# A chain of four modulated convolutions on one core: edge copies moved to ScalarE, the last iterations reordered on VectorE, the last product in two pieces, loads of X in three pairs

## The chip, the core and the metric

The kernel runs on one core of a Trainium2 chip. The metric is the device time of one execution in microseconds (us): the median of three runs, 475.31 us before the change (474.93 to 475.59). A core has a matrix engine (PE, with its weight loads shown apart as PEld), a vector engine (DVE, also VectorE), an activation engine (ACT, also ScalarE), a general engine (POOL, also GpSimd) and a sequencer for transfers (SP). Each has its own instruction queue, worked off in order; they wait for each other through semaphores.

## The reference, cut to what matters

Every batch element (128 of them, 64 channels by 1024 columns) goes through four modulated convolution layers (same, upsample by 2 with a blur, same, blur with downsample by 2), whose weights depend on a style vector of that element, and the result is added to the input.

```python
def _layer(x, style, w, b, mw, mb, typ):
    s = style @ mw.T + mb
    weight = SCALE * w * s[:, None, :, None]
    demod = lax.rsqrt(jnp.sum(weight * weight, axis=(2, 3)) + EPS)
    weight = weight * demod[:, :, None, None]
    ...
out = x
for i, typ in enumerate(('same', 'upsample', 'same', 'downsample')):
    out = _layer(out, style, weights[i], biases[i], mod_w[i], mod_b[i], typ)
x = x + out
```

## The kernel before

Four elements are worked on at a time: 32 quads q = 0..31 (`NQ`), two elements on the two halves of the 128 partitions, two pairs behind each other. The four layers are linear, so the kernel first makes one merged filter per element (small 64x64 matmuls: `stage1`, `stage2`, `stage3`, whose results pass through PSUM tiles psS, psR and psW into S, R and Wf) and then applies it to X. X is held in three planes (every third column, 344 columns each), and the filter is applied by five products over sums of planes, after the manner of a fast convolution. `product(q, m, ...)` is one of these: three taps, each as four matmuls on 64x64 quarters of the array and 342 columns (`NB`), written to a PSUM tile psA or, for product 4, to Y. A matmul of this type stands as two instructions in the program, so a product is 24 matmul rows on PE.

The parts of one quad that the change and the prediction speak of:

- Inputs, on DVE unless POOL is named: `in_g01` and `in_g2` make G from X (L715), `in3` makes the operand T3 (L764), `in04` the two operands T04 (L795, both pairs of elements in one instruction, or one with `PAIR[0]`/`PAIR[1]`), `in1` and `in2` the two operands T12 (L781, L786; on POOL except in the first and last quads).
- Weights on DVE: `combine_a`, `combine_b` (L715 and L712, tile H).
- Products in the order 3, 1, 2, 4, 0. `copy_m3` saves product 3 (ACT, L847), `sum1` makes y from product 1, `sum2` makes Y and y from product 2 (DVE), then product 4 accumulates in Y and product 0 in psA.
- `output(q, i, s)` scales plane i of pair s and adds the bias into the o tile (ACT, L887; one of the last two on DVE, L889), `store` sends it to HBM.
- The edge columns (three at each end of each element) are wrong in the merged form. They are computed apart, into Oe; `correct(q, planes)` copies the edge columns of o into Oc (POOL, L1169) for the first 27 quads, and `correct_all` subtracts Oe from all of these at once (DVE, L1178); for the later quads `correct` subtracts directly (L1171). `store_ends` sends Oc to HBM. `gather(q)` is `correct` for both groups of planes.

The order is written by hand (`tc.manual_schedule`): each engine gets its instructions in the order in which the Python code emits them, and waits are put in where the tiles' regions demand it. `early_turn(q)` does quads 0 to 3, `turn_of(q)` quads 4 to 28, and the code behind the loops quads 29 to 31. A turn works on several quads at once: products 2, 4 and 0 of q, products 3 and 1 of n = q+1, filter and inputs of c = q+2, the first filter stage of s = q+4. `load(c + 1, ...)` fetches X for q+3 through SP's queue, into one of two buffers; a store goes through the same queue. The transfers use eight semaphores (DMAHW0 to DMAHW7) in turn, so that a transfer waits first for the one eight before it.

At the start PE fills Y with zeros (`zeros_to_y`, L186: a zero weight times zeros), since products of the small filters accumulate there; the first matmuls on data (L223) need the parameters that the first transfers bring.

Of the kernel before, what the change touches and what calls it, by code (L numbers as in the profile page):

```python
# [55 lines left out]
K = 3  # L56
# [7 lines left out]
def kernel(  # L64
# [110 lines left out]
    NB = 342  # L175
# [618 lines left out]
            )  # L794
            nc_v.tensor_sub(t[:, pairs, :, :NJ], both(a, PL), both(b, 1))  # L795

    def product(q, m, ps, groups=range(K), alone=False):

        W, H_ = Wq[q]
        tag, i = SLOT[m]  # L800
        for g in groups:
            for s, rows in enumerate(HALF):
                for c, cols in enumerate(HALF):
                    if m in (0, 4):
                        w = W[rows, tap(m // 2, g), c, :]
                    else:
                        w = H_[rows, m - 1, g, c, :]
                    nc.tensor.matmul(  # L808
                        ps[s][cols, :NB],
                        w,  # L810
                        Ts[q, tag][rows, c, i, g : g + NB],
                        start=(g == 0 and (m == 3 or alone)),
                        stop=(g == K - 1),
                        skip_group_check=True,
                    )
# [12 lines left out]
    def banks(q):  # L828
        return A[q] if isinstance(A[q], list) else [A[q][:, s] for s in range(2)]
# [19 lines left out]
    def conv1(q, *groups):  # L849
        product(q, 1, banks(q), groups or range(K))  # L850
# [7 lines left out]
    def conv2(q, *groups):  # L858
        product(q, 2, banks(q), groups or range(K))
# [18 lines left out]
        nc_g.memset(t[:, :, :, NB:], 0.0)  # L878
    os = [t[:, :, :, :NB] for t in o_tiles] * (NQ // 2)

    def output(q, i, s, eng=nc_a):

        d3, add = td[:, q, s : s + 1], tb[:, q, s : s + 1]
        src = (banks(q)[s][:, :NB], y1w[q][:, s], Y[:, s, :NB])[i]
        dst = os[q][:, s, i]
        if eng is nc_a:
            nc_a.activation(dst, src, AF.Identity, bias=add, scale=d3)  # L887
        else:
            eng.tensor_scalar(dst, src, d3, add, op0=ALU.mult, op1=ALU.add)  # L889
# [270 lines left out]
        at, step = ((0, NB - 1), (0, NB - 2))[planes.start > 0]  # L1160
        return o[:, :, at : step + 1 : step, planes], 2 * q

    LATER_ENDS = NQ - 5

    def correct(q, planes, eng=nc_g):
        src, b = edges(q, planes)
        at = slice(b, b + 2)
        if q < LATER_ENDS:
            eng.tensor_copy(Oc[:, at, :, planes], src)  # L1169
        else:  # L1170
            eng.tensor_sub(Oc[:, at, :, planes], src, Oe[:, at, :, planes])  # L1171

    def gather(q):
        for planes in (slice(1, K), slice(0, 1)):
            correct(q, planes)

    def correct_all(n):
        nc_v.tensor_sub(Oc[:, : 2 * n], Oc[:, : 2 * n], Oe[:, : 2 * n])  # L1178
        store_ends(0, n)
# [13 lines left out]
    first = PART[0]  # L1193
    psB = [Y[:, r] for r in range(2)]
    zeros_to_y(2, 384, 6)
    zeros_to_y(2, 96, 1, False)
    nc_v.tensor_scalar_mul(mbs, mb, SCALE)
    mod_matmul(first, pm[0][0], (2,))
    nc_v.tensor_mul(wsq[T, 2], wio[2][T], wio[2][T])
    zeros_to_y(2, 256, 2, False)  # L1200
    nc_a.activation(
        ssq[:, 2, first],
        by_layer(pm[0][0], first)[:, 2],
# [137 lines left out]
    def last_factors():  # L1341
# [22 lines left out]
        14: lambda: (blur_side(0, 0), blur_side(1, 0)),  # L1364
        15: lambda: (blur_side(0, 1), blur_side(1, 1)),
        16: lambda: (blur_side(0, 2), blur_side(1, 2)),
        28: lambda: correct_all(LATER_ENDS),
    }

    def extra(*at):  # L1370
# [20 lines left out]
    def early_turn(q):  # L1391
        n, c, s = q + 1, q + 2, q + 3 + (q >= AHEAD)
        twice = q == AHEAD
        if q == 1:
            nc.sync.dma_start(Xe, x_ends)
        stage2(c)
        sum2(q)
        if q == 0:
            in_g01(n)
        if q == 1:  # L1400
            in_g2(n)
            load(n + NX)
        combine_a(n)
        combine_b(n, range(2 if q == 0 else 3))
        if q == 0:
            in_g2(n)
            load(n + NX)
        conv4(q)
        if q == 0:
            var_matmul(PART[1], var_of(PART[1]), start=False)  # L1410
            var_root(PART[1], var_of(PART[1]))
            in1(n, nc_v)
            in2(n, nc_v)
            combine_b(n, (2,))
# [36 lines left out]
        outputs(q, 1)  # L1451
        if q > 1:
            in_g2(c)
            if q < AHEAD:
                load(c + NX)
        extra(q, 1)
        sum1(n)
        if q == 0:
            in04(n)
        if q == 1:  # L1460
            in_g01(c)
        conv0(q, 1)
        if twice:
            stage1_a(s)
        else:
            stage1_b(s)
        if q == 0:
            table_3(PART[1])
            vector_Da(PART[1])
        conv0(q, 2)  # L1470
        for i in range(2):
            output(q, 0, i)
        conv2(n, 0)
        if twice:
            stage1_b(s)
        if q == 0:
            in_g01(c)
        if q == 1:
            in_g2(c)
            load(c + NX)  # L1480
        if q:
            in1(c, nc_g)
            in2(c, nc_g)
            gather(q - 1)
        extra(q, 2)
        scale3(s + 1)
        if q == AHEAD - 1:
            scale3(s + 2)
        conv2(n, 1, 2)
        for i in range(2):  # L1490
            store(q, i, slice(0, 1 if late(q) else K))

    def turn_of(q):
        n, c, s = q + 1, q + 2, q + 4
        entry = q == FIRST
        stage2(c)
        if entry:
            sum2(q)
            conv4(q)
            combine_a(n)  # L1500
            r_sums(c, nc_v)
        else:
            if q - 1 in SLOTS:
                SLOTS[q - 1][0](banks(q - 1))
            conv2(q)
            r_sums(c, nc_g)
            if q - 1 in SLOTS:
                SLOTS[q - 1][1](A[q - 1])
            sum2(q)
            in2(n, nc_g)  # L1510
        side(TABLES, q)
        for i in range(3):
            load(c + 1, slice(i, i + 1))
        stage3_b(c, open_a(n))
        if entry:
            conv0(q, 0, 1)
        else:
            combine_a(n)
            conv4(q)
        stage3_a(c)  # L1520
        combine_b(n)
        conv3(n)
        if entry:
            copy_m3(n)
            stage1_a(s)
        outputs(q, 2)
        if not entry:
            if s < NQ:
                stage1_a(s)
            copy_m3(n)  # L1530
        in04(n)
        if sharing(q):
            share_sums(c + 1)
        in_g2(c)
        side(SIDE, q)
        if q in SMALL:
            l, bs = SMALL[q]
            nc_v.memset(high(bs.stop - bs.start), 0.0)
        conv0(q, *((2,) if entry else range(K)))
        if entry:  # L1540
            conv1(n, 0, 1)
        outputs(q, 1)
        if s < NQ:
            stage1_b(s)
        in_g01(c)
        if sharing(q):
            share(c + 1, banks(q))
            share_copy(c + 1)
        outputs(q, 0)
        conv1(n, *((2,) if entry else range(K)))  # L1550
        if q in SMALL:
            small(q)
        sum1(n)
        in3(c)
        gather(q - 1)
        if s == NQ:
            in04(c)
        in1(c, nc_g)
        if s + 1 < NQ:
            scale3(s + 1)  # L1560
# [16 lines left out]
    conv3(n)  # L1577
    outputs(q, 2)
    copy_m3(n)
    in_g01(c)  # L1580
    in_g2(c)
    in3(c)
    stage3(c, 1)
    conv0(q, 0)
    conv1(n)
# [4 lines left out]
    conv0(q, 1, 2)  # L1590
    outputs(q, 0)
    for i in range(2):
        for planes in (slice(1, K), slice(0, 1)):
            correct(q - i, planes)
    conv2(n)
    sum2(n, (0,))
    combine_b(c, (1,))
    in1(c, nc_v)
    sum2(n, (1,))
    combine_b(c, (2,))  # L1600
# [47 lines left out]
        plus(i, o[:, i, 2], Y_banks, one_td, m3[:, i])  # L1648
        store(q, i, slice(2, K))
    correct(q, slice(1, K), nc_v)  # L1650
    conv0(q, *range(K))
    for i, (eng, queue) in enumerate(zip(BOTH, (nc_a, nc.sync))):
        output(q, 0, i, eng)
        store(q, i, slice(0, 1), queue)
    correct(q, slice(0, 1), nc_v)
    store_ends(LATER_ENDS, NQ)


# [74 lines left out]
```

## Time and profile before

| | |
|---|---|
| three runs | 474.93, 475.31, 475.59 us |
| the profiled execution | 475.6 us, of which the profile's span is 473.2 us |
| DVE, ACT, POOL busy | 414.8 us (88%), 311.3 us (66%), 186.0 us (39%) |
| DMA | 70.78 MB, mean 150 GB/s |
| granted TensorE clock | 0.998 |

The page gives for each engine its busy time, then the chain of work that ended last, then the costliest groups of instructions. In an answer of the timeline each row has a start in us, a duration in us, engine, line, operation, tile written and tiles read, form and count, and in brackets the idle time of the engine before it with what ended it. A row with a count merges instructions that follow each other; its start is the first one's. Ends of matmuls are modelled, so the pace of PE is read from start to start.

### The profile page before, as it was taken

How to read it: one execution, taken by the hardware profiler on the slowest of the kernel's cores; microseconds unless marked ns; L12 is line 12 of the kernel's file. 1: busy time of each engine (PE TensorE's matmuls, PEld its weight loads, DVE VectorE, ACT ScalarE, POOL GpSimd, SP SyncE). 2: the span in 40 equal slices, each digit the busy share in tenths (PEclk: the TensorE clock that was granted, in tenths of full speed). 3: DMA queues.
4: the chain of work that ended last, by engine and by line, in shares of the span. 5: the costliest groups of instructions: out<-in, count | busy, mean ns of one | idle time of the engine just before them, and what ended most of it. 6: DMA issues, size and time to landing. Idle time of an engine off the chain costs nothing. (4 is left out here: it accounts for less than half of the span.)

```text
span 473.2 us, 26920 instructions
## 1 busy us (share of the span) xinstructions
PE 466.0 (98%) x11996; PEld 343.0 (72%) x11996; DVE 414.8 (88%) x676; ACT 311.3 (66%) x711; POOL 186.0 (39%) x268
## 2 busy tenths in 40 slices
PE   9999999999999999999999999999999999999996
PEld 7987778777767779677877677766677676676653
DVE  5899989778989989998999987898898889889995
ACT  5566566577776667665777756687666777766364
POOL 4634241763448642243433333323334433243310
PEclk9999999999999999999999999999999999999999
DMA  5226444554445453344534545444555544455225
GB/s 178 93 96 212 165 158 145 153 158 139 157 152 157 153 181 126 122 153 153 158 133 153 167 124 176 145 150 151 143 175 161 180 138 149 142 154 160 98 91 183
DMA packets 52835, 70.78 MB, mean 150 GB/s; under 512 B 6128, under 2 KB 50928, under 8 KB 52720
## 3 DMA queue, kind: packets, MB, share of 16 engines
q1 hardware_dynamic: 52496, 68.84, 45.7%
q8 instruction: 94, 1.54, 1.4%
q14 instruction: 21, 0.17, 0.1%
q10 hardware_dynamic: 224, 0.23, 0.1%
HBM read 35.03 MB, written 34.01 MB: 146 GB/s over the span
## 5 line engine op out<-in xcount | busy, mean ns | idle before, releaser
L808 PE MATMUL psA<-T,H 64*64 64x342 f32 x2304 | 186.7, 448 | 0.0
L808 PEld LDWEIGHTS psA<-T,H 64*64 64x64 f32 x2304 | 88.9, 134 | 47.8 <-issue 2.1
L715 DVE SCALAR_TENSOR_TENSOR G<-X 128x1378 f32<-128x1378 f32 (+2 forms) x65 | 78.3, 1211 | 0.2
L487 POOL TENSOR_TENSOR S<-S 128x128 f32<-128x128 f32 x28 | 20.9, 745 | 140.1 <-ACT S L402 140.0
L781 POOL TENSOR_TENSOR T<-G 128x688 f32<-128x688 f32 x28 | 46.4, 1658 | 63.4 <-DVE G L715 59.4
L808 PE MATMUL Y<-T,Wf 64*64 64x342 f32 x768 | 62.6, 454 | 1.1 <-DVE Y L715 1.1
L808 PE MATMUL psA<-T,Wf 64*64 64x342 f32 x768 | 63.6, 448 | 0.0
L402 ACT ACTIVATE R<-psR,tC 128x448 f32<-128x448 f32 x63 | 36.5, 630 | 35.6 <-PE psR L509 20.8
L402 ACT ACTIVATE psW<-psA 128x128 f32<-128x128 f32 x100 | 19.3, 269 | 54.4 <-PE psA L624 50.3
L715 DVE SCALAR_TENSOR_TENSOR Y<-m,psA 128x342 f32<-128x342 f32 x62 | 32.2, 519 | 25.7 <-PE psA L808 24.6
L795 DVE TENSOR_TENSOR T<-G 128x1376 f32<-128x1376 f32 (+1 forms) x33 | 52.6, 1593 | 0.0
L402 ACT ACTIVATE Wf<-psW,t 128x256 f32<-128x256 f32 (+2 forms) x76 | 32.7, 480 | 29.1 <-PE psW L624 28.9
L764 DVE TENSOR_TENSOR T<-X 128x688 f32<-128x688 f32 x32 | 51.4, 1606 | 0.0
L786 POOL TENSOR_TENSOR T<-G 128x688 f32<-128x688 f32 x28 | 47.2, 1685 | 0.0
L509 PE MATMUL psR<-S,E 64*64 64x64 f32 (+1 forms) x1472 | 46.7, 238 | 0.0
L431 PEld LDWEIGHTS psS<-wd,w2n 64*64 64x64 f32 x1120 | 34.4, 133 | 13.4
L808 PEld LDWEIGHTS Y<-T,Wf 64*64 64x64 f32 x768 | 28.3, 132 | 20.5 <-DVE Y L715 1.3
L509 PEld LDWEIGHTS psR<-S,E 64*64 64x64 f32 x1472 | 38.9, 134 | 5.2 <-ACT psR L532 0.2
L887 ACT ACTIVATE o<-psA,tb,td 128x342 f32<-128x342 f32 x63 | 37.2, 651 | 5.0 <-PE psA L808 5.0
L808 PEld LDWEIGHTS psA<-T,Wf 64*64 64x64 f32 x768 | 29.0, 134 | 15.1 <-ACT m L1643 0.2
L887 ACT ACTIVATE o<-Y,tb,td 128x342 f32<-128x342 f32 x62 | 36.1, 641 | 4.8 <-PE Y L808 2.9
L887 ACT ACTIVATE o<-y,tb,td 128x342 f32<-128x342 f32 x62 | 38.6, 681 | 0.0
(186 smaller groups left out, 840.0 us busy)
## 6 DMA issues: line engine op xcount, KB each, us to landing
out<-o SPq DMA_DIRECT2D x191, 172.0 KB, 2.3
X<-in_x SPq DMA_DIRECT2D x150, 172.0 KB, 3.1
X<-in_x SPq DMA_DIRECT2D x14, 516.0 KB, 4.7
par<-in_params SPq DMA_DIRECT2D x3, 192.0 KB, 3.8
Xe<-in_x_ends SPq DMA_DIRECT2D x1, 192.0 KB, 3.8
out<-o ACTq DMA_DIRECT2D x1, 172.0 KB, 2.2
out<-Oc SPq DMA_DIRECT2D x1, 162.0 KB, 3.4
par<-in_params SPq DMA_DIRECT2D x1, 160.0 KB, 2.7
```

The source lines that it names most:

```text
L402: nc_a.activation(dst, src, AF.Copy, scale=f)
L431: nc.tensor.matmul(ps[r][cols, at * C : (at + n) * C], weight[rows], wd[c if r == 0 else 1 - c][rows, taps], start=first, stop=last, skip_ ...
L487: nc_g.tensor_add(t[:, :, 2], t[:, :, 2], t[:, :, 0])
L509: nc.tensor.matmul(dst[r][cols], weight[rows], st[c if r == 0 else 1 - c][rows, slots, :], start=False, stop=last, skip_group_check=True,)
L715: nc_v.scalar_tensor_tensor(out, x, f, y, op0=ALU.mult, op1=op)
L764: nc_v.tensor_sub(t[:, pairs, 0, :NJ], plane(X, 3, pairs), plane(X, 1, pairs))
L781: eng.tensor_add(t[:, :, 0, :NJ], plane(g, 2), plane(g, 1))
L786: eng.tensor_sub(t[:, :, 1, :NJ], plane(g, 2), plane(g, 1))
L795: nc_v.tensor_sub(t[:, pairs, :, :NJ], both(a, PL), both(b, 1))
L808: nc.tensor.matmul(ps[s][cols, :NB], w, Ts[q, tag][rows, c, i, g : g + NB], start=(g == 0 and (m == 3 or alone)), stop=(g == K - 1), skip_ ...
L887: nc_a.activation(dst, src, AF.Identity, bias=add, scale=d3)
```

## The change

Five edits in one:

1. `gather` for quads 0 to 25 is done by ACT (a copy), right behind the outputs of the same quad, and no longer by POOL one turn later. `LATER_ENDS` falls from 27 to 26, so quad 26 is subtracted directly, and `correct_all` comes in turn 27 instead of 28.
2. `load(c + 1, ...)`: the three pairs of transfers of a turn, which stood together near the start of the turn, stand apart: ahead of the outputs of plane 2, behind them, and behind those of plane 1.
3. DVE's order from turn 28 on: of `in04(30)` only the first pair stays in turn 28; `in3(31)` and the second pair of `in04(30)` come ahead of `in_g01(31)`, and `in_g2(31)` comes later, between two steps of `combine_b(31)`, ahead of `in1(31)`.
4. The last product (product 0 of quad 31) is done in two pieces: first the columns 0 to 87 and 254 to 341 ("sides", one access pattern with two runs of 88), with their outputs, stores, the last `correct` and `store_ends`, then the 166 columns between ("middle") with theirs.
5. The same number of zero columns is written to Y at the start in more and narrower matmuls: 96 columns in 3 pieces instead of 1, 256 in 4 instead of 2.

```diff
-    def product(q, m, ps, groups=range(K), alone=False):
+    WHOLE = slice(0, NB)
+    SIDES, MIDDLE = 88, slice(88, NB - 88)
+
+    def columns(v, at):
+        if at != SIDES:
+            return v[..., at]
+        ap = [list(d) for d in v.ap]
+        return bass.AP(v.tensor, v.offset, [*ap[:-1], [ap[-1][0] * (NB - SIDES), 2], [ap[-1][0], SIDES]])
+
+    def product(q, m, ps, groups=range(K), alone=False, at=WHOLE):
...
-                        ps[s][cols, :NB],
+                        columns(ps[s][cols], at),
                         w,
-                        Ts[q, tag][rows, c, i, g : g + NB],
+                        columns(Ts[q, tag][rows, c, i, g:], at),
...
-    def output(q, i, s, eng=nc_a):
+    def output(q, i, s, eng=nc_a, at=WHOLE):
...
-    LATER_ENDS = NQ - 5
+    LATER_ENDS = NQ - 6
...
-        if q < LATER_ENDS:
-            eng.tensor_copy(Oc[:, at, :, planes], src)
+        if eng is nc_a:
+            eng.copy(Oc[:, at, :, planes], src)
...
-            correct(q, planes)
+            correct(q, planes, nc_a if q < LATER_ENDS else nc_g)
...
-    zeros_to_y(2, 96, 1, False)
+    zeros_to_y(2, 96, 3, False)
...
-    zeros_to_y(2, 256, 2, False)
+    zeros_to_y(2, 256, 4, False)
...
-        28: lambda: correct_all(LATER_ENDS),
+        NQ - 5: lambda: correct_all(LATER_ENDS),
...
-        for i in range(3):
-            load(c + 1, slice(i, i + 1))
+        load(c + 1, slice(0, 1))
...
         outputs(q, 2)
+        load(c + 1, slice(1, 2))
...
         outputs(q, 1)
+        load(c + 1, slice(2, 3))
...
         outputs(q, 0)
+        if q < LATER_ENDS:
+            gather(q)
...
-        gather(q - 1)
+        if q > LATER_ENDS:
+            gather(q - 1)
         if s == NQ:
-            in04(c)
+            in04(c, PAIR[0])
...
     copy_m3(n)
+    in3(c)
+    in04(n, PAIR[1])
     in_g01(c)
-    in_g2(c)
-    in3(c)
...
     combine_b(c, (1,))
+    in_g2(c)
     in1(c, nc_v)
...
-    conv0(q, *range(K))
-    for i, (eng, queue) in enumerate(zip(BOTH, (nc_a, nc.sync))):
-        output(q, 0, i, eng)
-        store(q, i, slice(0, 1), queue)
-    correct(q, slice(0, 1), nc_v)
-    store_ends(LATER_ENDS, NQ)
+    for at in (SIDES, MIDDLE):
+        product(q, 0, banks(q), at=at)
+        for i, (eng, queue) in enumerate(zip(BOTH, (nc_a, nc.sync))):
+            output(q, 0, i, eng, at)
+            queue.dma_start(
+                columns(out[q, :, i, :NO], at), columns(o_tiles[q % 2][:, i, 0], at)
+            )
+        if at == SIDES:
+            correct(q, slice(0, 1), nc_v)
+            store_ends(LATER_ENDS, NQ)
```

The first place is DVE's queue at the end of turn 28 and in the code behind the loops (the rows between, which only make y, Y and H of quads 29 and 30, are left out by quoting two stretches). Before:

```order
L715 SCALAR_TENSOR_TENSOR G_8406<-X_102 128x2x344
L1178 TENSOR_TENSOR Oc<-Oc,Oe 128x324
L715 SCALAR_TENSOR_TENSOR G_8406<-X_102 128x2x689
L715 SCALAR_TENSOR_TENSOR y_29_8443<-psA_8310,m_29_8402 128x684
L764 TENSOR_TENSOR T_30_8445<-X_102 128x688
L795 TENSOR_TENSOR T_30_8449<-G_8406 128x1376
L715 SCALAR_TENSOR_TENSOR Y<-m_29_8402,psA_8310 128x342 x2
```

and now, on the same engine at the same place:

```order
L715 SCALAR_TENSOR_TENSOR G_8422<-X_102 128x2x344
L715 SCALAR_TENSOR_TENSOR G_8422<-X_102 128x2x689
L715 SCALAR_TENSOR_TENSOR y_29_8459<-psA_8324,m_29_8418 128x684
L764 TENSOR_TENSOR T_30_8461<-X_102 128x688
L795 TENSOR_TENSOR T_30_8465<-G_8422 128x688
L715 SCALAR_TENSOR_TENSOR Y<-m_29_8418,psA_8324 128x342 x2
```

Ahead of the Y of quad 29 stands one instruction fewer, and `in04` (L795) has half its columns. The second place is DVE's queue behind the Y of quad 30, where the inputs of the last quad are made; before:

```order
L715 SCALAR_TENSOR_TENSOR Y<-m_30_8576,psA_8559 128x342 x2
L715 SCALAR_TENSOR_TENSOR H_8510<-Wf_8509,H_8510 128x384
L781 TENSOR_TENSOR T_31_8657<-G_8578 128x2x344
L867 TENSOR_TENSOR y_30_8619<-y_30_8619,psA_8559 128x684
L715 SCALAR_TENSOR_TENSOR H_8510<-H_8510,Wf_8509 128x384
L786 TENSOR_TENSOR T_31_8657<-G_8578 128x2x344
L795 TENSOR_TENSOR T_31_8715<-G_8578 128x688
L1614 SCALAR_TENSOR_TENSOR y_31_8680<-psA_0_8662,times,m_31_8679 128x342
```

and now:

```order
L715 SCALAR_TENSOR_TENSOR Y<-m_30_8592,psA_8575 128x342 x2
L715 SCALAR_TENSOR_TENSOR H_8526<-Wf_8525,H_8526 128x384
L715 SCALAR_TENSOR_TENSOR G_8597<-X_103 128x2x344
L781 TENSOR_TENSOR T_31_8674<-G_8597 128x2x344
L877 TENSOR_TENSOR y_30_8635<-y_30_8635,psA_8575 128x684
L715 SCALAR_TENSOR_TENSOR H_8526<-H_8526,Wf_8525 128x384
L786 TENSOR_TENSOR T_31_8674<-G_8597 128x2x344
L795 TENSOR_TENSOR T_31_8732<-G_8597 128x688
L1628 SCALAR_TENSOR_TENSOR y_31_8697<-psA_0_8679,times,m_31_8696 128x342
```

The G of `in_g2(31)` has come in between. The third place is the end of the program, with the semaphores that each row waits for: first ACT's last rows before, then now.

```order
L887 ACTIVATE o_141<-psA_0_8662,tb,td 128x342 [waits DMAHW0_49,PE_49]
L892 DMA out<-o_141 128x344 [waits DMAHW4_49,Activation_49]
```

```order
L897 ACTIVATE o_141<-psA_0_8679,tb,td 128x2x88 [waits DMAHW0_49,PE_49]
L1669 DMA out<-o_141 128x2x88 [waits DMAHW4_49,Activation_49]
L897 ACTIVATE o_141<-psA_0_8679,tb,td 128x166 [waits DMAHW4_49,DVE_49,PE_49]
L1669 DMA out<-o_141 128x166 [waits DMAHW7_49,Activation_49]
```

Then DVE's last rows now (before, one row of 128x342 stood between the two of Oc):

```order
L1181 TENSOR_TENSOR Oc<-o_141,Oe 128x4x2 [waits DVE_49]
L899 TENSOR_SCALAR o_141<-psA_1_8680,td,tb 128x2x88 [waits DMAHW1_49,PE_49]
L1181 TENSOR_TENSOR Oc<-o_141,Oe 128x4 [waits DVE_49,Activation_49]
L899 TENSOR_SCALAR o_141<-psA_1_8680,td,tb 128x166 [waits DMAHW5_49,DVE_49,PE_49]
```

and SP's last transfers now:

```order
L1669 DMA out<-o_141 128x2x88 [waits DMAHW5_49,DVE_49]
L1193 DMA out<-Oc 128x72 [waits DMAHW6_49,DVE_49,Pool_49]
L1669 DMA out<-o_141 128x166 [waits DMAHW5_49,DMAHW0_49,DVE_49]
```

Each of the two last outputs has become two, and the second of each waits for the semaphore of a transfer that the first did not wait for. On PE the product's two pieces wait as follows:

```order
L818 MATMUL psA_0_8679<-T_31_8732,Wf_8525 64x2x88 [waits Activation_49]
L818 MATMUL psA_1_8680<-T_31_8732,Wf_8525 64x2x88 [waits DVE_49]
L818 MATMUL psA_0_8679<-T_31_8732,Wf_8525 64x166 [waits Activation_49]
L818 MATMUL psA_1_8680<-T_31_8732,Wf_8525 64x166 [waits DVE_49]
```

The middle's matmuls wait for ACT and for DVE a second time.

More of the change, by code (lines that the diff above doesn't have):

```diff
@@ L879 @@
     os = [t[:, :, :, :NB] for t in o_tiles] * (NQ // 2)
-    def output(q, i, s, eng=nc_a):
+    def output(q, i, s, eng=nc_a, at=WHOLE):
         d3, add = td[:, q, s : s + 1], tb[:, q, s : s + 1]
-        src = (banks(q)[s][:, :NB], y1w[q][:, s], Y[:, s, :NB])[i]
-        dst = os[q][:, s, i]
+        src = columns((banks(q)[s], y1w[q][:, s], Y[:, s])[i], at)
+        dst = columns(os[q][:, s, i], at)
         if eng is nc_a:
@@ L1549, in turn_of @@
         outputs(q, 0)
+        if q < LATER_ENDS:
+            gather(q)
         conv1(n, *((2,) if entry else range(K)))
@@ L1554, in turn_of @@
         in3(c)
-        gather(q - 1)
+        if q > LATER_ENDS:
+            gather(q - 1)
         if s == NQ:
-            in04(c)
+            in04(c, PAIR[0])
         in1(c, nc_g)
@@ L1592 @@
     for i in range(2):
-        for planes in (slice(1, K), slice(0, 1)):
-            correct(q - i, planes)
+        gather(q - i)
     conv2(n)
```

## The prediction

> **What bounds the kernel now.** I read the page's busy times first, then PE's waits, then a table of stretches, then the timeline of one turn, of the last three quads and of the first 5 us.
>
> ```profile
> span 473.2 us, 26920 instructions
> PE 466.0 (98%) x11996; PEld 343.0 (72%) x11996; DVE 414.8 (88%) x676; ACT 311.3 (66%) x711; POOL 186.0 (39%) x268
> ```
>
> PE is busy for all but 7.2 us of the span. Its waits, in the order of their sum:
>
> ```profile
> PE Y L808 <- DVE Y L715: 1.1, 1, 1.1
> PE Y L186 <- DVE eps L156: 1.0, 1, 1.0
> PE psW L624 <- issue: 0.8, 2, 0.6
> ```
>
> There are three, together 2.9 us; the rest is the stretch behind PE's last matmul. By stretch (length, then busy time of PE, PEld, DVE, ACT, POOL):
>
> ```profile
> 418.50:432.40 13.90, 13.90 (x392) 9.77 (x384) 12.11 (x19) 8.88 (x21) 5.07 (x7) 1.00 0.48 149
> 432.40:447.17 14.77, 13.66 (x281) 9.24 (x273) 14.54 (x18) 8.51 (x19) 5.34 (x5) 1.00 0.39 129
> 447.17:458.50 11.33, 11.32 (x168) 6.58 (x172) 10.92 (x20) 4.85 (x9) 1.42 (x4) 1.00 0.27 95
> ```
>
> In a turn of the loop (first row) PE is never idle, at full clock. In the second row, which runs into quad 29, it lacks 1.11 us: that is the wait for Y. So an edit pays only there, in the first microseconds, or behind the last matmul; elsewhere it can only do harm.
>
> **The loop: edge copies and loads, 0 us.** One turn in the timeline:
>
> ```profile
> 384.90 1.19 ACT L887 ACTIVATE o<-psA,tb,td 128x342 f32<-128x342 f32 x2
> 387.89 1.16 ACT L402 ACTIVATE R<-psR,tC 128x448 f32<-128x448 f32 x2 [0.91 <-PE psR L509]
> 389.35 0.94 PE L624 MATMUL psA<-R,w0s 64*64 64x192 f32 x24
> 2.60 0.20 ACT L158 ACTIVATE one<-one 128x1 f32<-128x1 f32 x1
> L402 ACT ACTIVATE psW<-psA 128x128 f32<-128x128 f32 x100 | 19.3, 269 | 54.4 <-PE psA L624 50.3 <-issue 4.1
> ```
>
> The two copies of 8 and 4 columns come behind the outputs of plane 0 (first row). No such copy on ACT is in the trace; it lies between the 0.20 us of one column and the 0.27 us of 128, nearer the first: 0.4 to 0.54 us a turn, and with a wait of each for its predecessor's end perhaps 0.7. Queued behind them are the two copies of wd and then R, ahead of which ACT idles 0.91 us until PE delivers psR: that idle time is the cover. Were it gone, PE would wait for R only after another 0.30 us (R ends at 389.05, its matmuls start at 389.35). POOL loses the work, but no wait of PE ends on POOL. So 0; if the copies cost 1.5 us instead, some 0.3 us in each of 22 turns.
>
> The loads move behind stores in SP's queue:
>
> ```profile
> 382.40 0.87 DVE L715 SCALAR_TENSOR_TENSOR G<-X 128x688 f32<-128x688 f32 x1
> 383.20 1.25 ACT L887 ACTIVATE o<-y,tb,td 128x342 f32<-128x342 f32 x2
> 386.53 4.53 SPq L147 DMA_DIRECT2D X<-in_x  x6
> X<-in_x SPq DMA_DIRECT2D x150, 172.0 KB, 3.1
> ```
>
> The six transfers are issued at the start of a turn, for a quad whose first reader (`in_g2`, as at 382.40) comes two periods of 13.90 us later, at 410.2. Moved behind the outputs of plane 1 (second row, one period later: 397.1 to 398.4) the last pair is issued by 399.2 and lands 3.1 us after that: still 8 us early. The stores between are late by the issue of one pair, about 0.8 us, and their tile is written again two turns later. 0 us.
>
> **DVE's order at the end, -0.6 us.**
>
> ```profile
> 445.12 0.94 PE L624 MATMUL psW<-R,w0s 64*64 64x128 f32 x24
> 443.09 3.04 DVE L795 TENSOR_TENSOR T<-G 128x1376 f32<-128x1376 f32 x1
> 446.05 1.06 DVE L715 SCALAR_TENSOR_TENSOR Y<-m,psA 128x342 f32<-128x342 f32 x2
> 447.17 1.96 PE L808 MATMUL Y<-T,Wf 64*64 64x342 f32 x24 [1.11 <-DVE Y L715]
> 438.62 0.49 DVE L1178 TENSOR_TENSOR Oc<-Oc,Oe 128x324 f32<-128x324 f32 x1
> 436.15 1.58 DVE L795 TENSOR_TENSOR T<-G 128x1376 f32<-128x1376 f32 x1
> 461.35 0.87 DVE L795 TENSOR_TENSOR T<-G 128x688 f32<-128x688 f32 x1
> ```
>
> PE's wait for Y (fourth row) has ahead of it on DVE the whole `in04(30)`, 3.04 us beside POOL's work where the same form alone takes 1.58. Half of it saves 1.58 - 0.87 = 0.71; without `correct_all` (0.49) the queue starts up to that much earlier. Y is then done 0.7 to 1.2 us earlier, and PE can start when its own work ahead ends, 445.12 + 0.94 = 446.06: gain 1.1, the whole wait (0.7 at the least). What is late next is the queue behind the Y of quad 30:
>
> ```profile
> 450.90 2.37 DVE L715 SCALAR_TENSOR_TENSOR G<-X 128x1378 f32<-128x1378 f32 x2
> 426.12 1.58 DVE L715 SCALAR_TENSOR_TENSOR G<-X 128x1378 f32<-128x1378 f32 x1
> 458.53 0.87 DVE L781 TENSOR_TENSOR T<-G 128x688 f32<-128x688 f32 x1
> 462.30 1.06 DVE L1614 SCALAR_TENSOR_TENSOR y<-psA,times,m 128x342 f32<-128x342 f32 x2
> 463.71 1.93 PE L808 MATMUL psA<-T,H 64*64 64x342 f32 x24
> ```
>
> `in_g2(31)` costs 2.37 - 1.58 = 0.8 us and now stands there, ahead of `in1` (third row), and I allow 0.1 for `in1`, which now waits for its predecessor's end. DVE has no gap from there to the y of quad 31, which ended at 463.36; product 2 of that quad overwrites its psA and started at 463.71. Of the 0.9 us, 0.35 is slack, and 0.5 becomes a new wait of PE. Net -0.6; ends 0 (0.7 gained, and the new wait no smaller) and -1.1 (no new wait).
>
> **The last product in two pieces, +1.9 us.** Before:
>
> ```profile
> 468.97 0.17 DVE L1171 TENSOR_TENSOR Oc<-o,Oe 128x8 f32<-128x8 f32 x1
> 469.12 0.64 ACT L887 ACTIVATE o<-psA,tb,td 128x342 f32<-128x342 f32 x1 [2.24 <-PE psA L808]
> 469.18 0.63 DVE L889 TENSOR_SCALAR o<-psA,td,tb 128x342 f32<-128x342 f32 x1
> 470.28 0.40 SPq L1183 DMA_DIRECT2D out<-Oc  x1
> out<-Oc SPq DMA_DIRECT2D x1, 30.0 KB, 2.0
> DMA to landing us min/median/max: 1.8/2.0/2.5
> ```
>
> The last row is for the ten transfers from 463 us on. The last one issued lands at 470.28 + 2.0 = 472.28, and the program ends 0.94 us later. The intent of two pieces is that the sides' outputs and stores run while PE does the middle. The order's rows forbid it. ACT issues the sides' store behind a wait for DMAHW4, and its very next output, the middle's, waits for DMAHW4 again: an engine has no need to wait twice for one count, so the second is the count that this store adds when it lands. DVE's middle output waits in the same way for DMAHW5, the semaphore of SP's store of the sides, and PE's middle matmuls wait a second time for ACT and DVE. The sides' access pattern spans columns 0 to 341, which holds the middle: the program takes the two for overlapping. So the middle may not be written before the sides have landed.
>
> From 469.18: sides 0.46 us (0.63 less 166 columns at the 342's rate of about 1 ns, so that 176 remain), issue 0.03, landing 2.0, then 0.05, middle 0.45, issue 0.03, landing 2.0: 469.18 + 5.02 = 474.20, against 472.28: +1.9. With 1.8 us for both landings +1.5, with 2.5 for both +2.9. PE's middle (half a product, whose row lasts 1.93 us) is over before the first landing, and ACT's half is earlier, since its sides don't queue behind the Oc row. [...] The sides' runs are 352 B. The trace shows no cost of that: Oc with runs of 240 B landed in 2.0 us, like the stores of 172 KB. [...]
>
> **More zeros, +0.1 us.**
>
> ```profile
> 0.97 1.58 PEld L186 LDWEIGHTS Y<-Z 64*64 64x64 f32 x56 [0.97 <-DVE eps L156]
> 2.77 0.29 PEld L223 LDWEIGHTS psM<-par_s 128*64 128x64 f32 x4 [0.22 <-DMA par_s<-in_params_s]
> 3.18 0.73 PEld L186 LDWEIGHTS Y<-Z 64*64 64x64 f32 x16
> 4.13 0.22 PEld L258 LDWEIGHTS psM<-ssq,q 64*64 64x64 f32 x4 [0.22 <-issue]
> ```
>
> 56 rows at 28 ns fill PE until 2.55, and the parameters arrive 0.22 us later; 16 more rows cost 0.45 less what narrower ones save, so they overrun by up to 0.23. The second lot, 16 rows at 46 ns, becomes 32 at 28 (+0.17) ahead of another gap of 0.22. Together 0.40 - 0.22: between 0 and 0.2 late at 4.13, from which the start's chain of dependent steps goes on. A gain is not in sight, since the columns are the same.
>
> **Sum.** 0 - 0.6 + 1.9 + 0.1 = +1.4 us. The profiled execution took 475.6 us (2.4 outside its span) and would take 477.0; it lies 0.3 above the median of the runs shown, so the median goes to 475.31 + 1.4 = 476.7 us.
>
> **The rivals.**
>
> *The pieces overlap after all* (not slower). If the second waits were for counts long reached, as DVE's for DMAHW1 ahead of its sides is, the sides are out at 469.64, their store and Oc's leave SP by 470.4, the middle's is issued at about 470.45 and lands at 472.45, +0.2, and with the other terms -0.3: 475.0. It decides if the middle's output waits less than about 0.5 us. For it: ACT's output before also waited for a transfer (DMAHW0), and its 2.24 us ended with PE's product, not with that. Against it: the repeated wait on ACT. 0.11.
>
> *The loads in pairs free the code's own fetches.* PE's 0.8 us of "issue" in L624 are waits for nothing that the profile shows; if they come from the traffic of six loads at once and go with it, and the pieces overlap as well, 475.0 - 0.8 = 474.2. Nothing in the rows ties them to the loads. 0.06.
>
> *ACT's copies push R* beyond PE's product: 22 turns at 0.1 to 0.3 us, +2 to +7 on top: 479 to 483. It begins when the two copies exceed 0.91 + 0.30 = 1.2 us; twice the dearest near row is 0.54. 0.09.
>
> **How the numbers follow.** The forecast has 0.74. Its own range from the bounds: -1.1 + 1.5 + 0 = +0.4 to 0 + 2.9 + 0.2 = +3.1, 475.7 to 478.4; both ends need every term at its end. For 8 in 10 over all cases I take 475.4 to 478.0. A difference of 0.2% (0.95 us) is about what can be told from none: of the forecast's 0.74, 0.64 lies above 476.26 and 0.10 below; with the third rival slower is 0.73. Same: 0.10 + 0.08 of the first rival = 0.18. Faster: 0.06 + 0.03 of the first rival = 0.09.
>
> **What would show it.** The landing: DVE's last output of 166 columns with some 2 us idle ahead, ended by a transfer of o, and the chain of waits ending in it instead of in PE. The DVE order: product 4 of quad 29 without its 1.11 us, and a wait of about 0.5 us ahead of product 2 of quad 31. The loop: periods of 13.90 us as before, R still waiting for PE. Wrong it would be if DVE's last two outputs stand within 1 us of each other, or if a turn's period is longer.

## The result, and the profile after

The changed kernel took 483.8 us (median of five runs, 483.1 to 485.5) where the kernel before took 475.6 beside it: a ratio of 1.0167, 95% interval 1.0146 to 1.0187, or +7.9 us. The prediction was 476.7 (475.4 to 478.0): slower, as forecast, but by more than five times as much (+1.4 predicted). The profiled execution took 485.45 us, of which the span is 483.6. Its page:

```profile
span 483.6 us, 26990 instructions
PE 473.0 (98%) x12052; PEld 378.1 (78%) x12052; DVE 414.5 (86%) x678; ACT 319.0 (66%) x764; POOL 174.2 (36%) x216
DMA out<-o 1%; DVE o L1628 0%; DVE o L899 0%; DVEq L899 0%; DVE Oc L1181 0%
q8 instruction: 94, 1.54, 1.4%
out<-o SPq DMA_DIRECT2D x190, 172.0 KB, 2.7
X<-in_x SPq DMA_DIRECT2D x150, 172.0 KB, 3.7
```

The third row is the chain that ended last: it now runs through a landing of o, as forecast. But that landing is 0.6% of the span. In the last two rows the transfers are slower: the median landing of an X load went from 3.1 to 3.7 us, that of a store from 2.3 to 2.7. And PEld is busy for 35 us more, with 56 weight loads more.

The waits of the changed kernel (engine, tile, line and what ended them: sum, times, longest), those of PE, PEld and the last outputs:

```profile
PE psA L818 <- DVE Ve L1136: 1.5, 1, 1.5
PE psA L624 <- issue: 1.1, 3, 0.5
PE psR L509 <- issue: 0.9, 3, 0.5
PEld Y L818 <- issue: 2.2, 4, 0.8
PEld psA L624 <- issue: 2.2, 5, 0.7
PEld psA L818 <- POOL R L641: 1.7, 1, 1.7
PE psA L818 <- ACT o L897: 0.4, 1, 0.4
DVE o L899 <- DMA out<-o: 2.6, 1, 2.6
```

The wait for Y of quad 29 is gone. New are the tail's waits (last two rows) and, in the loop, more waits for "issue", that is for nothing that the profile shows. They look small, but a table of stretches shows where the time went. Three turns of the changed kernel (length, then busy time of PE, PEld, DVE, ACT, POOL, clock, share of the transfers, GB/s):

```profile
342.09:356.62 14.53, 14.03 (x383) 11.39 (x382) 12.46 (x20) 10.02 (x25) 4.87 (x5) 1.00 0.50 149
371.07:385.13 14.06, 14.06 (x385) 13.71 (x385) 11.67 (x19) 10.12 (x25) 4.01 (x5) 1.00 0.50 147
208.94:226.06 17.12, 15.65 (x421) 11.09 (x416) 13.62 (x22) 10.08 (x25) 5.47 (x5) 1.00 0.44 135
```

Each stretch runs from one quad's product 4 to the next quad's, and I name the turn by the later one: 22, 24 and 13. A turn that took 13.90 takes 14.53 and 14.06, and turn 13 took 15.44 before. From the first product 4 (31.14 us) to that of quad 28 the changed kernel needs 410.2 us, the one before 403.3 (29.07 to 432.41): between these two profiles 6.9 us of the loss lie in the loop, which I had priced at nothing.

### The profile page after: what moved, and what is told of

Read it like the earlier page. It is cut to its first block, busy times and chain, and to the rows that moved or that the text cites. A ratio compares the mean times of both kernels' runs of the same rounds, so it can differ in the third digit from the quotient of the medians.

```text
span 483.6 us, 26990 instructions
## 1 busy us (share of the span) xinstructions
PE 473.0 (98%) x12052; PEld 378.1 (78%) x12052; DVE 414.5 (86%) x678; ACT 319.0 (66%) x764; POOL 174.2 (36%) x216
## 3 DMA queue, kind: packets, MB, share of 16 engines
q8 instruction: 94, 1.54, 1.4%
## 5 line engine op out<-in xcount | busy, mean ns | idle before, releaser
L818 PE MATMUL psA<-T,H 64*64 64x342 f32 x2304 | 191.2, 449 | 1.6 <-DVE Ve L1136 1.5
L818 PEld LDWEIGHTS psA<-T,H 64*64 64x64 f32 x2304 | 105.2, 133 | 37.3 <-issue 2.1
L818 PE MATMUL psA<-T,Wf 64*64 64x342 f32 (+2 forms) x792 | 66.2, 439 | 0.6 <-ACT o L897 0.4
L795 DVE TENSOR_TENSOR T<-G 128x1376 f32<-128x1376 f32 (+1 forms) x34 | 52.7, 1550 | 0.0
L509 PE MATMUL psR<-S,E 64*64 64x64 f32 (+1 forms) x1472 | 50.2, 238 | 0.7 <-issue 0.7
L509 PEld LDWEIGHTS psR<-S,E 64*64 64x64 f32 x1472 | 45.1, 134 | 4.2 <-issue 0.9
L818 PEld LDWEIGHTS Y<-T,Wf 64*64 64x64 f32 x768 | 34.0, 132 | 16.6 <-issue 2.2
L431 PEld LDWEIGHTS psS<-wd,w2n 64*64 64x64 f32 x1120 | 38.9, 133 | 9.8
L818 PEld LDWEIGHTS psA<-T,Wf 64*64 64x64 f32 x792 | 34.8, 133 | 12.4 <-ACT o L897 0.7
L897 ACT ACTIVATE o<-psA,tb,td 128x342 f32<-128x342 f32 (+1 forms) x64 | 37.6, 646 | 7.1 <-PE psA L818 4.2
L624 PEld LDWEIGHTS psA<-R,w0s 64*64 64x64 f32 x1000 | 35.2, 134 | 3.9 <-issue 0.6
```

Of the source, the lines that this page charges most:

```text
L431: nc.tensor.matmul(ps[r][cols, at * C : (at + n) * C], weight[rows], wd[c if r == 0 else 1 - c][rows, taps], start=first, stop=last, skip_ ...
L509: nc.tensor.matmul(dst[r][cols], weight[rows], st[c if r == 0 else 1 - c][rows, slots, :], start=False, stop=last, skip_group_check=True,)
L624: nc.tensor.matmul(dst[r][cols], weight[rows], t[rows, c, slots, :], start=first, stop=last, skip_group_check=True,)
L818: nc.tensor.matmul(columns(ps[s][cols], at), w, columns(Ts[q, tag][rows, c, i, g:], at), start=(g == 0 and (m == 3 or alone)), stop=(g == ...
```

## What the code's fetches show

The transfer queue "instruction" of the page (q8: 94 transfers, 1.54 MB, so 16 KB each) brings PE's code, as I read it: PE has 12,052 matmuls and as many weight loads, 24,104 in all and so 256 to a transfer. I set PE's stalls inside the loop (over 0.14 us, read from start to start) beside the number of the instruction that came late, counted from the first (with PE's 126 waits and 3 drains), modulo 256, and beside the end of the last such transfer. Some of the 18 stalls of the changed kernel:

```
stall us           length  instruction mod 256   last code transfer, us
145.81 -> 146.11   0.30    194                   143.05 - 144.69
221.18 -> 222.92   1.74    195                   220.34 - 221.24
279.52 -> 280.18   0.66    193                   277.87 - 278.79
355.87 -> 356.62   0.75    193                   354.42 - 355.34
412.82 -> 413.19   0.37    193                   410.68 - 411.57
```

All stalls stand at the same place in a block of 256 instructions (190 to 195), and end 1.2 to 1.7 us after a block has landed (a few fall in two parts, the first ending 0.8 to 0.9 us after it). The reverse holds too: between 100 and 445 us the changed kernel passes this place 72 times and the kernel before 73 times, never less than 1.2 us after the last landing, and where the block landed early there is no stall. I read this as PE having run out of code. The five loop stalls of the profile before (its two "issue" waits of L624 among them) stand at 193 and 194 too: 2.0 us in sum, against 8.3 us now. The stall of 1.74 us, which the list of waits lays to DVE and POOL, is one of them: the work named had simply ended last. Of the 72 code transfers between 100 and 445 us, 12 start when PE has fewer than 140 instructions left to that place; of 73 before, 5. What else moves then are X and the outputs: in the kernel before a short block of stores and, after a pause, the rest of the stores and then the six loads; in the changed kernel loads and stores in turn, in one stretch from about 5 to 13 us of a turn. So far this is a reading of traces. The runs tested it. Where I speak of the phase, I mean where in a turn the place 193 falls; a turn is three blocks long, so the phase stays from turn to turn until other code comes in. In both kernels the transfer of a block starts 51 to 292 instructions ahead of the place where it is needed.

## The experiments

Each kernel was run beside the one before on the same chip; ratios carry their 95% interval, and a difference in us is the ratio's distance from 1 times 475. The first four are the edits alone.

**Loads in pairs alone.**

```diff
-        for i in range(3):
-            load(c + 1, slice(i, i + 1))
+        load(c + 1, slice(0, 1))
...
         outputs(q, 2)
+        load(c + 1, slice(1, 2))
...
         outputs(q, 1)
+        load(c + 1, slice(2, 3))
```

> The kernel before, with the six loads of a turn issued as three pairs and nothing else. Theory 'late code': in the changed kernel PE's new stalls in the loop (0.2 to 0.75 us each, released by nothing that the profile shows) follow fetches of PE's code that start late, because the pairs and the stores between them make one unbroken block of transfers; then this edit alone carries the loop's loss: +4 to +6 us, 479.5 to 481.5, periods of 14.0 to 14.6 us in turns 14 to 28, and PE's issue waits 3 us or more in sum. Rival 'late R' (the two copies on ACT): no change here, 475.0 to 476.0 and periods of 13.90. Rival 'both together': below +2 here and below +2 for the copies alone.

Measured 479.0 us, 1.0086 (1.0069 to 1.0102): +4.1 us. The periods of turns 21 to 27 are 13.94 to 14.35, as in this row of its stretches:

```profile
350.82:365.08 14.26, 14.26 (x392) 12.52 (x385) 12.06 (x19) 9.80 (x23) 4.81 (x7) 1.00 0.50 156
```

This is turn 23. PE shows as busy throughout: its modelled ends swallow a stall of 0.22 us at 352.7. The weight loads tell it: they are spread over 12.5 us in place of 9.8, which I read as PE running close to the end of its code. Eleven stalls, 4.9 us, all at 192 to 194 of a block. The size is that of "late code", but PE's list of waits gives only 1.9 us of them as "issue" where I expected 3 or more, and the stalls are not in every turn from 14 on.

**Edge columns on ACT alone.**

```diff
-        if q < LATER_ENDS:
-            eng.tensor_copy(Oc[:, at, :, planes], src)
+        if eng is nc_a:
+            eng.copy(Oc[:, at, :, planes], src)
```

> The kernel before, with the edge columns copied by ACT (and correct_all one turn earlier) and nothing else. 'Late code': 475.0 to 476.0, periods of 13.90. 'Late R': 479 to 481, with PE waiting for R in some 20 turns. 'Both together': below 477.5 here and for the loads alone.

Measured 473.7 us, 0.9976 (0.9962 to 0.9990): -1.1 us, faster than any of the theories had it. "Late R" falls. ACT's rows of one turn:

```profile
384.55 0.37 ACT L1169 COPY Oc<-o 128x8 f32<-128x8 f32 x2
384.82 1.01 ACT L402 ACTIVATE wd<-w3x,tA 128x320 f32<-128x320 f32 x2
386.49 1.16 ACT L402 ACTIVATE R<-psR,tC 128x448 f32<-128x448 f32 x2 [0.66 <-PE psR L509]
```

A pair of copies holds the next row up by 0.27 us, and ACT still idles 0.66 us ahead of R. Of the gain, 0.4 us is PE's wait for Y of quad 29 (its period is 14.36 in place of 14.75): `correct_all` has left that turn.

**The last product in two pieces alone.**

```diff
+    for at in (SIDES, MIDDLE):
+        product(q, 0, banks(q), at=at)
```

> The kernel before, with the last product in two pieces and nothing else. Theory 'a landing in between': +1.9 as predicted, +2.6 if the landings last as long as in the changed kernel: 477.2 to 478.1, with DVE's last output idle 2.0 to 2.7 us until a transfer of o lands. Rival 'the pieces overlap': 475.3 to 475.8.

Measured 477.2 us, 1.0041 (1.0026 to 1.0056): +1.9 us.

**More zeros alone.**

```diff
-    zeros_to_y(2, 96, 1, False)
+    zeros_to_y(2, 96, 3, False)
...
-    zeros_to_y(2, 256, 2, False)
+    zeros_to_y(2, 256, 4, False)
```

> The kernel before, with the zeros of Y in more and narrower matmuls and nothing else. The changed kernel's profiled run was 2.1 us late at the first product (31.14 against 29.07), and its matmuls kept the slow pace until about 8 us where those of before were at the fast pace from about 4.7. Theory 'the zeros cause it': 477 to 478, in all runs. Rival 'it varies by itself from run to run': 475.3 to 476.0 in the median, with single runs of this kernel and of the one before up to 2 us apart and a lower granted clock in the longer ones. My prediction's term was +0.1 (0 to 0.2).

Measured 475.6 us, 1.0017 (1.0004 to 1.0030): +0.8 us. The time lies in the rival's range, but the kernel before ran at 474.8 beside it, so a small cost is left. Most of the 2.1 us by which the changed kernel's profile was late is chance. The 32 rows of the first blur matmuls show it, in the kernel before, in the changed one, and in the kernel with pieces apart (below), whose start is that of before:

```profile
4.69 1.32 PE L382 MATMUL Y<-par,idb 64*64 64x192 f32 x32
```

```profile
5.13 2.41 PE L382 MATMUL Y<-par,idb 64*64 64x192 f32 x32
```

```profile
4.86 2.41 PE L382 MATMUL Y<-par,idb 64*64 64x192 f32 x32
```

With one and the same code at the start they took 1.32 to 2.41 us in nine profiles, and quad 0's product 4 came at 29.07 to 30.41; with more zeros, in five profiles, at 29.44 to 31.14. The profile of before happened to be the earliest of all.

**Loads in pairs and more zeros**, then **loads in pairs and copies on ACT**: the diffs above, two at a time.

> The kernel before with loads in pairs and the zeros in more matmuls. The single edits measured +4.2 and +0.8 on 474.8. Theory 'late code, by phase': PE's code arrives in blocks of 256 instructions, a turn holds about three of them, and the 64 instructions that the zeros add move the turn against the blocks, so that another fetch meets the pairs' transfers: more than the sum, 481 to 483, with issue waits in nearly each turn from 14 on, as in the changed kernel. Rival 'additive': 479.5 to 480.1, and the loop's periods as with the loads alone (14.2 to 14.35 in turns 21 to 27, 13.9 in most others).

Measured 481.2 us, 1.0141 (1.0117 to 1.0165): +6.7 us, where the two alone make +4.9. The 14 loop stalls make 7.8 us, the longest 1.94.

> The kernel before with loads in pairs and the edge columns copied by ACT. The single edits measured +4.2 and -1.0. 'Late code, by phase': neither moves PE's code, so they add up: 477.5 to 478.5. Rival 'both together' (ACT's copies delay the stores that the pairs stand behind): 480 to 482, periods like the changed kernel's 14.1 to 14.7 from turn 19 on.

Measured 477.4 us, 1.0053 (1.0032 to 1.0075): +2.5 us, and the two alone make +3.0. So not the copies but the zeros make the paired loads dearer, by 1.8 us, which is just outside the intervals of the three runs (about 1.5 together).

**The changed kernel with its loads together again** (the first diff undone).

> The changed kernel with the six loads of a turn issued together again, as before; everything else as changed. 'Late code': the loop's loss goes, periods of 13.90 again, and what is left is copies -1.0, pieces +2.4, zeros +0.8 and DVE's order about -0.6: 476.0 to 477.0. Rival 'another edit makes half of the loss': 478 to 480.

Measured 476.1 us, 1.0031 (1.0016 to 1.0047): +1.5 us. Two loop stalls are left, 0.6 us. The loads' share of the changed kernel is 7.9 - 1.5 = 6.4 us.

**DVE's order alone.**

```diff
-            in04(c)
+            in04(c, PAIR[0])
...
-    in_g2(c)
-    in3(c)
+    in3(c)
+    in04(n, PAIR[1])
...
     combine_b(c, (1,))
+    in_g2(c)
```

> The kernel before with DVE's new order from turn 28 on and nothing else (correct_all stays in turn 28). Predicted term -0.6, ends -1.1 and 0; without the move of correct_all the gain of 1.1 shrinks to some 0.7 and the new wait of 0.5 ahead of product 2 of quad 31 stays: 474.3 to 474.8 against 474.8. Rival 'no new wait': 473.7 to 474.1.

Measured 474.2 us, 0.9987 (0.9972 to 1.0001): -0.6 us, a little more than expected of this edit with `correct_all` left in its place (474.3 to 474.8), and the interval reaches no change. Its one wait of PE past the first us:

```profile
PE Y L808 <- DVE Y L715: 0.4, 1, 0.4
```

**Loads in pairs with fewer zeros**, and **fewer zeros alone**: PE's code shifted by 64 instructions the other way.

```diff
-    zeros_to_y(2, 384, 6)
+    zeros_to_y(2, 384, 3)
...
-    zeros_to_y(2, 256, 2, False)
+    zeros_to_y(2, 256, 1, False)
```

> The kernel before with loads in pairs and FEWER zero matmuls at the start (384 columns in 3 pieces instead of 6, 256 in 1 instead of 2), which takes 64 instructions out of PE's code, as many as the more zeros add. Theory 'late code, by phase': in the loads-alone run the three fetches of a turn became due about 0.9, 6.7 and 10.2 us into the turn and waited 1.5 to 2.7 us; 64 instructions less move them to about 2.3, 7.1 and 10.9 us, where the first finds no traffic and the others have up to 0.7 us less of it ahead: issue stalls of 0 to 0.1 us in turns 19 to 27, loop loss 0 to 1.5 us instead of 4.2, 474.4 to 476.4. Rival 'phase is no matter': +4.2 as with the loads alone, 478.3 to 479.3.

Measured 479.9 us, 1.0102 (1.0080 to 1.0124): +4.8 us, far outside what I expected. Yet the turns for which I had worked it out came as expected. Two stretches of it, turns 15 and 23:

```profile
239.52:254.48 14.96, 14.03 (x393) 12.56 (x388) 12.88 (x21) 9.78 (x23) 4.86 (x6) 1.00 0.46 145
354.09:367.99 13.90, 13.90 (x392) 9.77 (x384) 12.11 (x19) 9.78 (x23) 5.07 (x7) 1.00 0.52 167
```

Turns 19 to 27 have no stall over 0.14 us. The loss moved to turns 8 to 17: eight stalls, 6.4 us. Between lie turns with edge matmuls, which add code and so shift the block against the turn once more; I had carried the phase of the last turns over to all. The phase has a say in where the stalls fall, and in the three phases tried the paired loads lost in one part of the loop or another. It isn't alone in this: loads in pairs with copies on ACT have the phase of the loads alone, and their stalls stand partly in other turns (none in 21 and 22, one in 19).

> The kernel before with FEWER zero matmuls at the start and nothing else. Theory 'each zero matmul costs': the more zeros measured +0.8, so as many fewer give -0.3 to -0.8: 474.1 to 474.6. Rival 'the narrow ones alone are at fault': 474.9, no change; rival 'fewer matmuls let PE fall idle and get its fast pace later': 475.5 to 477.

Measured 474.3 us, 0.9992 (0.9978 to 1.0005): -0.4 us, not told from no change. No stall in the loop.

**The last product in pieces that do not overlap.**

```diff
+    LEFT, RIGHT, MIDDLE = slice(0, 88), slice(NB - 88, NB), slice(88, NB - 88)
...
+    for part in ((LEFT, RIGHT), (MIDDLE,)):
+        for at in part:
+            product(q, 0, banks(q), at=at)
```

> The kernel before with the last product in pieces whose regions do not overlap: columns 0 to 87, 254 to 341 and 88 to 253 as three runs, each with matmuls, outputs and stores of its own. Theory 'the overlapping pattern makes the last outputs wait for a landing': the wait of 2 us on DVE is gone, and what is left is 24 more matmul rows and two more stores ahead of the last: 474.7 to 475.7, against 477.2 for the two pieces. Rival 'two steps of store cost two landings in any case': 476.8 to 477.6.

Measured 475.8 us, 1.0024 (1.0011 to 1.0037): +1.1 us. The landing is out of the way, in DVE's last rows and PE's:

```profile
469.57 1.17 PE L814 MATMUL psA<-T,Wf 64*64 64x166 f32 x24 [1.36 <-ACT o L893]
468.98 0.64 DVE L895 TENSOR_SCALAR o<-psA,td,tb 128x88 f32<-128x88 f32 x2
470.79 0.45 DVE L895 TENSOR_SCALAR o<-psA,td,tb 128x166 f32<-128x166 f32 x1 [0.90 <-PE psA L814]
```

What remains is a wait of PE for ACT, 1.36 us: its middle matmuls write the psA tile that ACT has just been reading, other columns of it.

**ACT copies and DVE's order together** (their diffs above).

> The kernel before with the edge columns copied by ACT and DVE's new order at the end: the two edits that measured faster alone (-1.0 and -0.7). Additive: 473.0 to 473.5, and the wait of PE for Y of quad 29 gone entirely. Rival 'both gain from the same wait of PE for Y' (correct_all's 0.49 us and half of in04): -1.0 to -1.2 in sum, 473.7 to 473.9.

Measured 473.7 us, 0.9974 (0.9961 to 0.9986): -1.2 us (a gain of 0.7 to 1.9), the rival's value: both draw on the one wait for Y, which is gone from PE's waits. The interval reaches the additive -1.7 as well, so the time alone does not decide it.

By then the cause lay in the loads, but their traffic and their place among the stores were still one. **Loads in pairs, more zeros, and the loop's loads left out** (the diff is against the kernel with pairs and more zeros); then **six loads together, but later in the program**:

```diff
-        load(c + 1, slice(0, 1))
...
-        load(c + 1, slice(1, 2))
...
-        load(c + 1, slice(2, 3))
```

> The kernel with loads in pairs and more zeros (481.2, stalls of 0.2 to 1.9 us in most turns from 10 on), with the loads of X in turns 4 to 28 left out, so that these quads work on old data; PE's code is the same. Theory 'the traffic of X delays the code': no stalls of over 0.3 us in the loop, periods of 13.90 in turns 19 to 27, 474.0 to 476.0. Rival 'something else in PE's code or in the stores': stalls stay, 479 or more.

Measured 476.6 us, 1.0020 (1.0001 to 1.0040): +1.0 us instead of +6.7. One loop stall over 0.14 us is left, of 0.4 us. Its turn 23, with 80 GB/s instead of some 150:

```profile
349.37:363.27 13.90, 13.90 (x393) 9.77 (x385) 12.12 (x19) 9.80 (x23) 5.08 (x7) 1.00 0.23 80
```

The median is 0.6 us above what I expected; I had not counted what more zeros cost without any loads in pairs, +0.8 alone.

```diff
         outputs(q, 1)
+        for i in range(3):
+            load(c + 1, slice(i, i + 1))
```

> The kernel before with the six loads of a turn still together, but issued behind the outputs of plane 1, where the last pair stands in the changed kernel. Theory 'one unbroken stretch of transfers, with a fetch due early in it': the fetch that is due about 10.2 us into the turn then stands behind six loads and the stores of plane 1 and waits over 3 us: stalls in turns 19 to 27, periods over 14.2, 478 to 486. Rival 'it is the alternation of loads and stores in pairs': 13.90, 474.5 to 475.5.

Measured 476.1 us, 1.0015 (0.9995 to 1.0035): +0.7 us, with an interval that reaches no change. The stalls that my theory expected did not come; the rival's 13.90 came, and its time nearly. Its turn 23, and its page's row of the loads with the median landing:

```profile
347.92:361.82 13.90, 13.90 (x392) 9.77 (x385) 11.74 (x19) 9.80 (x23) 5.07 (x7) 1.00 0.54 172
X<-in_x SPq DMA_DIRECT2D x150, 172.0 KB, 4.0
```

As much traffic, in one block and with slower landings (4.0 us, against 3.5 with the pairs alone), but only two loop stalls, of 0.5 us each. So slow landings are not enough. But the edit moved the traffic less than it seems to: each load comes nearly a whole turn later, and so lands at nearly its old place in a turn. Counted from product 4, the six are issued at 8.4 to 11.2 us, now ahead of the last two stores; in the kernel before at 9.7 to 13.8, behind them; with the pairs alone at about 5, 8 and 11, between the stores. So the stalls come with the traffic of X as the pairs place it. Whether it is the alternation with the stores or the earlier start that makes them is not shown, nor why the code waits longer there.

The loop's length in the profiles, from the first product 4 to that of quad 28, parts the kernels in the same way: 406.2 to 410.2 us in the five with pairs, 400.9 to 403.3 us in the twelve without. The kernel before is the longest of the twelve; the kernel with DVE's order alone, whose loop is the same, took 401.4. So the loop stalls of one profile are those of one execution, and such a profile tells a loop's time to about 2 us.

**The parts that gain: ACT copies, DVE's order, fewer zeros.**

> The kernel before with the edge columns on ACT, DVE's new order at the end and fewer zero matmuls: the parts that measured below 1.0 alone or together (0.9974 and 0.9992). Additive: 0.9966, 473.0 to 473.6. Rival 'they don't add, since the zeros move the code against the loop': 473.7 to 474.9.

Measured 473.1 us, 0.9940 (0.9920 to 0.9961): -2.8 us against the kernel before. The medians differ by 2.0 us only, since the runs of before scattered more than elsewhere (473.4 to 477.9). Its median is the lowest of all kernels run, and within what I expected of the sum. Its list of PE's waits has one row, the first wait of the program:

```profile
PE Y L186 <- DVE eps L156: 1.0, 1, 1.0
```

## Why the prediction was wrong

- **The loop's loads, 0 us: the step that failed.** I asked whether the data would land in time (it did) and whether the stores would be late. I did not ask what else comes by the same transfer engines (both pages put the queue "instruction" at 1.4% of the time of the 16). Alone the edit costs +4.1 us, in the changed kernel 6.4, because, as I read the stalls, code blocks come late. The sign of this was in the profile: "issue" waits of 0.8 us in L624, for which I had written that nothing in the rows ties them to the loads. They lie a multiple of 256 instructions apart, which the rows do show once they are counted. My second rival had the mechanism, as I read it, and the wrong sign: pairs do not free the code's path, they crowd it (pairs and more zeros cost +6.7 us, the same with the loop's loads left out +1.0).
- **The copies on ACT, 0 us: right on ACT, and a gain was left out.** The copies delayed ACT by 0.27 us a turn (I had 0.4 to 0.54) and R's cover held, so the third rival fell. The edit measured -1.1 us. The 0.4 us from moving `correct_all` I had counted with DVE's order; for the rest no wait was found, and whether there is one stays open.
- **DVE's order, -0.6 us: the mechanism right.** The wait for Y went to 0 with `correct_all` moved, 0.4 without. A new loss ahead of quad 31's product 4 is there, though no row names it a wait: quad 30's period is 11.47 to 11.49 in place of 11.37, and quad 31's 7.11 in place of 6.90, 0.3 us in sum against the 0.5 predicted. That leaves 1.1 - 0.3 = 0.8 gained, 0.4 of it by `correct_all`, which the runs count with the copies. By time the edit adds only -0.1 to the copies (-1.2 against -1.1), so the intervals neither confirm nor deny the -0.6.
- **Two pieces, +1.9 us: right**, +1.9 alone, and the first rival fell. DVE's last rows in the changed kernel:

```profile
477.23 0.46 DVE L899 TENSOR_SCALAR o<-psA,td,tb 128x176 f32<-128x176 f32 x1
480.53 0.45 DVE L899 TENSOR_SCALAR o<-psA,td,tb 128x166 f32<-128x166 f32 x1 [2.56 <-DMA out<-o]
```

  The first landing took 2.7 us and the last one 1.7, where I had 2.0 for each, so that two errors nearly cancel; 2.7 lies beyond the end that I gave, 2.5. With regions apart the wait is gone, which settles that the overlapping pattern makes it.
- **More zeros, +0.1 us: too small alone**, +0.8 (0.2 to 1.4). The first matmuls of L258 come at 4.36 us in place of 4.09 to 4.16, 0.2 to 0.3 us late, just past the end I gave. Where the rest comes from stays open.
- **Sum.** The four terms other than the loads give -1.1 - 0.6 + 1.9 + 0.8 = +1.0 alone, or +1.5 with the -1.2 that the first two measured together; the changed kernel without the pairs has +1.5, and predicted was +1.4. That this sum came so close is partly luck: the copies and DVE's order together gained 0.6 more than predicted (-1.2), the zeros cost 0.7 more. What is missing is the loads' 6.4.

## What to carry to other kernels

Here PE's program is, as I read the traces, itself a stream of transfers: 16 KB for every 256 instructions, three in a turn of 13.90 us or one each 4.6 us. A change that moves transfers, or lengthens the program ahead of a loop, is to be checked against it too: count the instructions between "issue" waits, and where they come to multiples of the block, ask what is in the queues when the next block is due. Price a new write pattern by the region it spans, not by the elements it touches: here the second piece waited 2.56 us for the landing of the first, whose two runs of 88 columns lie on both sides of it.

## What the runs showed of the hardware

- A late block of code, as I read it, stops PE until 1.2 to 1.7 us after it has landed, at the same instruction of each block (190 to 195 of 256 in the 18 loop stalls of the changed kernel); the list of waits calls it "issue", or names whatever other work ended last (1.74 us put to DVE and POOL). A rise of PEld's busy time with no more weight loads (9.77 us for 384 in a turn of the kernel before, 13.71 for 385 in turn 24 of the changed one) goes with turns in which PE, as I read it, runs at the end of its code.
- PE's pace at the start varies between executions of the same code: L382's 32 rows took 1.32 or 2.41 us, while the granted clock of both stretches reads 1.00:

```profile
4.69:5.94 1.25, 1.25 (x37) 1.04 (x33) 0.93 (x6) 0.43 (x3) 0.73 (x3) 1.00 0.82 201
```

```profile
4.86:7.50 2.64, 2.64 (x40) 2.02 (x40) 1.27 (x8) 1.19 (x4) 0.81 (x3) 1.00 0.90 310
```

  (the kernel before and the one with pieces apart). From the first start to the last these 32 rows take 1.05 us in the kernel before and 2.00 us in the changed one, whose row also has 2.41 us; in the seventeen profiles the fast pace sets in between about 4.7 and 8.7 us. What sets that moment was not shown.
